# A three-layer max-aggregating graph network: one-hots of layer 1 on VectorE as well, and another price for the lists' picking

## The chip, the cores and the metric

One NeuronCore of a Trainium2 chip runs the kernel. The metric is the device time of one execution in microseconds (us). The time of the kernel before is the median of three runs; the profile is one further execution, taken by the hardware profiler, and times from it are given in us from the start of its span.

## The reference

```
h = max(layernorm(x), 0)                       # 6250 nodes x 128
for Wl, bl, Wr in three layers:                # 128 -> 256 -> 256 -> 128
    agg = segment_max(h[src], dst)             # 200000 edges, sorted by dst; no edge: 0
    h = leaky_relu(agg @ Wl + bl + h @ Wr, 0.01)
out = x + h
```

The destinations are drawn as 6250 u², so low node numbers have many edges and high ones few.

## The kernel before, in words

The 6,250 nodes lie in 50 tiles of 127. An edge's source is a tile and a row in it. The kernel does most of the gathering of source rows as matrix products. For each group of destination nodes (`GROUPS`, five of them, k = 0 to 4) and each pair g of source tiles (25 pairs, from the last to the first), it knows for every destination one source row in that pair, as a byte (`idx_sb`, the same row of bytes on all partitions). A **one-hot** (`hot`) of 128 partitions by up to 1,024 destinations has a 1 where the byte names the partition. TensorE multiplies the tile pair (`pair_sb`) with it and puts the gathered rows into PSUM (`pg`, three buffers); VectorE takes the maximum into the accumulator (`acc`, L956). Edges that don't fit this scheme, a second source in the same pair above all, go to **lists** (k = 0 to 3, of depth 24, 24, 48, 24): GpSimd gathers their rows from DRAM by indirect DMAs (L988, with a pacing memset at L992 behind each), VectorE takes their maxima (L1003, L1008), and the result is fetched when a tile is finished (`agg`, L1033).

**Steps.** The work is one list of steps, 225 of them in layer 1 (called `layer == 0` in the code), 400 in each later layer. A step is one group, one pair, and up to 1,024 destinations. In layer 1 the groups follow each other: steps 0 to 74 are group 0, 75 to 124 group 1 (alternately 1,024 and 384 wide), 125 to 174 group 2, 175 to 199 group 3, all 1,024 wide, and 200 to 224 group 4, 512 wide. A step has two halves, s = 0 and 1, one for each tile of the pair (for groups 1 to 3 each half has its own `pg` and its own maximum). For each half `one_hot` makes, in layer 1, the **distance** `away` = |byte - partition's own number| as bytes (L916), from it the one-hot `relu(1 - away)` (L920), and stores the distance to DRAM in `far` (L922, a DMA on ScalarE's queue), from where the two later layers read it. All three are ScalarE's. There are six `hot` buffers (`HOTS`) and three `away` buffers.

**Order.** The order on each engine is the program's own. The main loop goes over t; it emits the one-hots of step t and the products and maxima of step t - 1. In iteration t there come, in this order: the index words for later gathers (`let`, L977) and the outputs of finished nodes; the first one-hot; the products of half 0 and, for groups 1 to 3, its maximum; the chores and list maxima (`MAXIMA`); the stages of nodes; the gathers and node fetches on GpSimd; the second one-hot; the products and the maximum of half 1. `act(...)` emits what `plan(t, rank, f)` has put down for t.

**Chores.** Layer 1 also prepares what the later groups and lists need, on VectorE, in pieces that `spread` deals over stretches of steps in proportion to a cost given with each piece: `stops` holds the stretches, 0 to 52, 52 to 104, 104 to 140 and 140 to 172. In the second stretch `late_rows(2)` prepares list 2 (16 units, in two parts of 8): masking and flagging each part, **picking** four units at a time (`pick_rows`: MAX8 at L555 and MATCH_REPLACE8 at L557, one round for each 8 of the list's depth), then `rank_rows` (VectorE L569 to L613 with three small products), 16 indirect DMAs on GpSimd that send the picked rows to DRAM (`picks`, L621), and a load of the whole list on SyncE's queue (`ell`, L631). Behind them `late_lookups` makes the bytes of group 2 in fifteen **expansions** (L719 to L726). The list's first gather stands at step 89.

**Nodes.** When group 0 is done, its 24 tiles are finished one a step from step 76 on: `agg` is fetched by GpSimd, `hT_in` by SyncE's queue, three steps later TensorE transposes `agg` (L1049), VectorE merges it (`mz`, L1055), TensorE multiplies by the weights (L1062, L1064), ScalarE copies (L1066, L848, L851), VectorE finishes (L1073, L856). Group 1 follows in the same way from step 126 on, the others after step 200.

Of the kernel before, what the change touches and what calls it, by code (L numbers as in the profile page):

```python
# [38 lines left out]
AF = mybir.ActivationFunctionType  # L39
OP = mybir.AluOpType  # L40
# [20 lines left out]
DEEP = (24, 24, 48, 24)  # L61
# [2 lines left out]
HOT, HOTS = 1024, 6  # L64
AHEAD = 3
EARLY = 44


@with_exitstack
def kernel(ctx: ExitStack, tc: tile.TileContext, x, src, dst,  # L70
                    Wl1, bl1, Wr1, Wl2, bl2, Wr2, Wl3, bl3, Wr3, out):
    nc = tc.nc
# [392 lines left out]
    def rows_of(us):  # L465
        w, i = us[0]
        assert [u for u in us] == [(w, i + j) for j in range(len(us))]
        return {"n": rows_n, "w": rows_w, "x": rows_x}[w][:, i : i + len(us), :]
# [8 lines left out]
    def width_of(us):  # L477
        w, i = us[0]
        ns = {WINDOW[j >= 24] if w == "n" else 2 * CUT if j < NW else CUT for w, j in us}
        return max(ns)  # L480
# [66 lines left out]
    def pick_rows(k, i0, us, S):  # L547

        n, W, m = len(us), width_of(us), DEEP[k]
        whole = S(0, F32, n, W)  # L550
        nc.vector.tensor_copy(whole, rows_of(us)[:, :, :W])
        top = S(2, F32, n, m)
        for i in range(n):
            for o in range(0, m, 8):
                nc.vector.max(out=top[:, i, o : o + 8], in_=whole[:, i, :])  # L555
                if o + 8 < m:
                    nc.vector.match_replace(  # L557
                        out=whole[:, i, :], in_to_replace=top[:, i, o : o + 8], in_values=whole[:, i, :], imm_value=0.0
                    )
        nc.vector.tensor_scalar(picked[k][:, i0 : i0 + n, :], top, -float(LEAF), 0.0, op0=OP.add, op1=OP.max)  # L560
        there = S(0, F32, n, m)
        nc.vector.tensor_scalar(there, top, float(LEAF), None, op0=OP.is_ge)
        nc.vector.reduce_sum(left_n[k][:, i0 : i0 + n], there, axis=AX.X)
# [65 lines left out]
    def load_ell(k):  # L629
        n = len(LISTS[k])  # L630
        nc.sync.dma_start(ell[k], picks[k].rearrange("(p q) m -> p q m", q=n))  # L631
# [141 lines left out]
    wr, wl, bias, bias3 = [], [], [], []  # L773
# [33 lines left out]
    near = keep.tile([P, 2], F32, name="near")  # L807
# [98 lines left out]

    hots, live, done_with = {}, [0], [0, 0]

    def one_hot(layer, k, g, c, w, odd, s):

        t, of = idx_q[layer, k, g]
        put = 2 * c * P + s * w
        if layer == 0:
            at = of + (c + (odd if s else 0) + (NV if PLANES[k][c] in EXTRA else 0)) * P
            away = work.tile([P, HOT], U8, tag="away", name="away", bufs=3)[:, :w]
            nc.scalar.activation(away, t[:, at : at + w], AF.Abs, bias=near[:, s : s + 1], scale=1.0)  # L916
        else:
            away = t[:, of + put : of + put + w]
        hot = work.tile([P, HOT], F32R, tag="hot", name="hot", bufs=HOTS)
        nc.scalar.activation(hot[:, :w], away, AF.Relu, bias=1.0, scale=-1.0)  # L920
        if layer == 0:
            nc.scalar.dma_start(far[k][:, g, put : put + w], away)  # L922
        hots[layer, k, g, c, s] = hot
        live[0] += 1
# [205 lines left out]
    def parts_in(layer, ks):  # L1130

        n = (8 if widths[layer] == P else 4) * P
        parts = []
        for k in ks:
            mine = list(parts_of(k))
            for i, (c0, pw, odd) in enumerate(mine):
                kind = PLANES[k][c0][0]
                cs = []
                for c in range(c0, c0 + pw // P, n // P):
                    w = min(n, (c0 - c) * P + pw)  # L1140
                    cs.append((c - (NV if kind == "x" else 0), w, c, PLANES[k][c][1] if kind == "w" else None))
                parts.append(((i + 0.5) / len(mine), k, (c0, pw, odd), cs))
        return [p[1:] for p in sorted(parts, key=lambda p: p[:2])]

    steps, begins, ends_at, order, blocks, jobs_h = [], [], {}, [], [], []
    for layer in range(3):
        begins.append(len(steps))
        for n, ks in enumerate(PASSES[layer]):
            for g in range(NG - 1, -1, -1):
                order.append((layer, n, g))  # L1150
                of = {}
                for k, (c0, pw, odd), cs in parts_in(layer, ks):
                    if k not in of:
                        if (NG - 1 - g) % GB[k] == 0:
                            blocks.append((layer, k, list(range(g, g - GB[k], -1))))
                        of[k] = max(i for i, b in enumerate(blocks) if b[:2] == (layer, k))
                    jobs_h += [(len(steps), of[k], (layer, k, g, c0, pw, odd, s)) for s in range(2)]
                    for c in cs:
                        steps.append((layer, k, g, c, n))
                        ends_at[layer, k] = len(steps)  # L1160
# [19 lines left out]
    chores = []  # L1180
# [4 lines left out]
    def late_rows(k):  # L1185
        us = LISTS[k]
        i0 = 0
        for part in [[u for u in us if (u in EXTRA_OF) == v] for v in (True, False)]:
            if not part:
                continue  # L1190
            chores.append((2.5, lambda part=part: mask_rows(part, S_acc)))
            chores.append((18 if part[0][0] == "w" else 6, lambda part=part: flag_rows(part, S_acc)))
            for i in range(0, len(part), 4):
                chores.append((7, lambda k=k, i0=i0 + i, p=part[i : i + 4]: pick_rows(k, i0, p, S_acc)))
            i0 += len(part)
        chores.append((7, lambda: rank_rows(k, S_acc, made)))
        for i in range(0, len(us), 4):
            chores.append((0, lambda i=i: [send_row(k, j) for j in range(i, min(i + 4, len(us)))]))

        def load():  # L1200
            load_ell(k)
            listed_at[k] = here_now[0]

        chores.append((0, load))
# [35 lines left out]
    i0 = 0  # L1240
    for i1, t0, t1 in stops:
        spread(chores[i0:i1], t0, t1)
        i0 = i1
# [5 lines left out]
    for layer in range(3):  # L1249
        b0, end = begins[layer], begins[layer + 1]  # L1250
        lists_ = [early_list if (layer, k) == (0, 0) else Listed(layer, k) for k in range(NL)]
        early = 0 if layer else EARLY
        turn = ends_at[layer, 3] - DELAY[layer]
        whens = []
        for part, t0, t1 in ((lists_[:3], max(b0 + 2, rows_at), turn), (lists_[3:], turn, end - 1 - SOON)):
# [5 lines left out]
            early, t = 0, 0  # L1261
# [4 lines left out]
        done_at, i, at = [], 0, 0  # L1266
        for k, li in enumerate(lists_):
            for t in range(len(li.seq)):
                if whens[i] is None:
                    at = 1 + i // 8  # L1270
                else:
                    plan(max(whens[i] - LEAD, 0), LET, lambda li=li, t=t: li.release(t))
                    plan(whens[i], GATHER, lambda li=li, t=t: li.gather(t))
                    at = max(at, whens[i] + (SOON if k == NL - 1 else DELAY[layer]))
# [83 lines left out]
    soon = early_list  # L1358
    for t in range(EARLY):
        soon.release(t)  # L1360
# [16 lines left out]
    for t in range(max(max(agenda)[0] + 1, len(steps) + 1)):  # L1377
# [10 lines left out]
        if t < len(steps):  # L1388
            st = steps[t]
            layer, k, _, _, _ = st  # L1390
            if (layer, k) not in accs:
                i, o = ACC[k]
# [10 lines left out]
        if before_:  # L1403
            p = psum.tile([P, 2, 512], F32, tag="pg", name="pg", bufs=3)
            products(before_[0], 0, p)
            if before_[0][3][3] is not None:
                maxima(before_[0], 0, p, accs[before_[0][:2]])
                p = psum.tile([P, 2, 512], F32, tag="pg", name="pg", bufs=3)
# [8 lines left out]
        if here and (t == 0 or pair_at(t - 1) != pair_at(t)):  # L1417
            i = at_pair[pair_at(t)] + 2
# [288 lines left out]
```

## Time and profile before

| | us |
|---|---|
| median of three runs (lowest, highest) | 3393.74 (3389.39, 3394.82) |
| the profiled execution: time, and its span | 3386.89, 3384.8 |
| busy over the span: PE, DVE, ACT, POOL | 2535.2, 2674.5, 1879.2, 2461.2 |
| layer 1's steps: first distance, last distance | 234.4, 1361.3 |
| ScalarE's distances (x450) and one-hots of layer 1 (x450) | 463.7, 427.7 |

PE is TensorE, PEld its weight loads, DVE VectorE, ACT ScalarE, POOL GpSimd, SP SyncE; a q behind a name is the engine's sequencer, which waits and issues DMAs. A group's row gives the source line, the engine, the operation, output and inputs with their shapes, the count, then the busy time, the mean of one in ns, and how long the engine idled just ahead of them and for whom. A timeline row gives start, duration, engine, line, names, and in brackets the idle time ahead with the releaser. A row of waits gives who waited for whom, the total, the number of times and the longest.

Steps are found in the trace by counting distances, two a step: step 52 begins its distances at about 490 us, step 75 at 610.9, step 125 at 909.5, step 145 at 1013.9, step 200 at 1255.4. VectorE's maximum of a step comes some steps' time behind that where VectorE is late.

### The profile page before, as it was taken

To read this page: it belongs to the slowest core of one execution; us is meant where nothing else is said; L and a number is where in the kernel's file an instruction comes from. 1 tells how busy PE (TensorE), PEld (TensorE's weight loads), DVE (VectorE), ACT (ScalarE), POOL (GpSimd) and SP (SyncE) were. 2 spreads that over 40 slices of the span, in tenths; PEclk is the share of its full clock that TensorE was granted. 3 is DMA by queue.
4 is the path that set the end of the run, shared out by engine and by line. 5 is a ranking of instruction groups with operands and counts; after the bars stand their busy time and mean duration, and the time that the engine had idled before them with its cause. 6 is when DMAs were issued, how large, how long until landed. Compare 5 with 4: busy or idle time off the path is not lost.

```text
span 3384.8 us, 38792 instructions
## 1 busy us (share of the span) xinstructions
PE 2535.2 (75%) x9920; PEld 1833.9 (54%) x9920; DVE 2674.5 (79%) x4157; ACT 1879.2 (56%) x2762; POOL 2461.2 (73%) x3478
## 2 busy tenths in 40 slices
PE   1035664365676667899999989887999999989886
PEld 1023333243454333677777666655777777666654
DVE  6677679777766653699989888884699989999974
ACT  5128897466999996555544434433455545333432
POOL 4788865476867655488888767775388888878782
PEclk9986777587778876899999999998999999999998
DMA  9234554267676677656757767667666756666575
GB/s 303 50 65 135 140 140 134 82 199 195 164 223 172 191 210 206 187 183 199 195 175 187 225 201 226 203 190 241 210 194 194 202 176 179 203 188 206 171 228 166
DMA packets 355527, 620.98 MB, mean 183 GB/s; under 512 B 68694, under 2 KB 216883, under 8 KB 354657
## 3 DMA queue, kind: packets, MB, share of 16 engines
q1 hardware_dynamic: 210561, 367.36, 33.7%
q0 software_dynamic: 79872, 199.22, 24.1%
q10 hardware_dynamic: 64864, 51.83, 4.5%
q8 instruction: 83, 1.36, 0.2%
q14 instruction: 147, 1.20, 0.1%
HBM read 476.03 MB, written 142.13 MB: 183 GB/s over the span
## 4 chain that ended last, share of the span: by engine, by line
PE 28%; DVE 22%; POOL 16%; DMA 12%; issue 11%; ACT 10%; SPq 0%; ACTq 0%; DVEq 0%; POOLq 0%
PE pg L939 21%; DVE acc L956 10%; POOL g L988 9%; ACT away L916 6%; DMA g<-table,let 5%; POOL pace_t L992 3%; ACT hot L920 3%; DVE g L1008 2%; PE z_p L1062 2%; DVE g L1003 2%; PE z_p L1064 2%; POOL picks L621 2%; DMA far<-away 1%; DMA joined<-joined_v 1%; DVE acc L557 1%
## 5 line engine op out<-in xcount | busy, mean ns | idle before, releaser
L939 PE MATMUL pg<-hot,pair_sb 128*128 128x512 f32 x8000 | 2212.9, 426 | 425.3 <-ACT hot L920 191.3
L939 PEld LDWEIGHTS pg<-hot,pair_sb 128*128 128x128 f32 x8000 | 1551.0, 204 | 950.8 <-ACT hot L920 422.2
L988 POOL DMA_INDIRECT g<-table,let x1539 | 1552.1, 1009 | 664.5 <-ACT let L977 291.0
L956 DVE TENSOR_TENSOR acc<-acc,pg 128x1024 f32<-128x1024 f32 (+3 forms) x1439 | 1642.8, 1167 | 415.0 <-PE pg L939 388.7
L920 ACT ACTIVATE hot<-idx_sb 128x1024 fp32r<-128x1024 uint8 (+1 forms) x900 | 817.1, 946 | 552.7 <-PE pg L939 349.2
L992 POOL MEMSET pace_t<- 128x300 bf16 x1539 | 563.0, 366 | 0.8
L916 ACT ACTIVATE away<-idx_sb,near 128x1024 uint8<-128x1024 uint8 (+2 forms) x450 | 463.7, 1030 | 68.4 <-DMA best<-g 17.7
L920 ACT ACTIVATE hot<-away 128x1024 fp32r<-128x1024 uint8 (+2 forms) x450 | 427.7, 950 | 46.0 <-PE pg L939 31.8
L1066 ACT COPY s<-z_p 127x256 f32<-127x256 f32 (+1 forms) x150 | 50.2, 334 | 452.0 <-PE z_p L1064 421.0
L1003 DVE TENSOR_TENSOR g<-g 128x1024 f32<-128x1024 f32 (+5 forms) x218 | 221.4, 1016 | 20.4 <-DMA g<-table,let 20.2
L1033 POOL DMA_INDIRECT agg<-best,end_i x141 | 144.7, 1026 | 106.9 <-PE aT_p L1049 41.2
L1008 DVE TENSOR_TENSOR g<-g 128x512 f32<-128x512 f32 (+3 forms) x351 | 173.1, 493 | 10.5 <-DMA g<-table,let 0.2
L1062 PE MATMUL z_p<-wr,hT_in 128*128 128x256 f32 (+1 forms) x500 | 142.9, 404 | 6.6 <-DMA hT_in<-across 6.6
L1064 PE MATMUL z_p<-wl,mz 128*128 128x256 f32 (+1 forms) x500 | 127.7, 373 | 14.6 <-DVE mz L1055 13.8
L846 PE MATMUL hT_p<-ident,h 128*128 128x128 f32 x200 | 47.9, 326 | 116.2 <-DVE mz L1055 54.1
L977 ACT ACTIVATE let<-ell 128x4 int32<-128x4 int16 (+3 forms) x444 | 81.1, 191 | 79.1 <-DMA ell<-picks 67.7
L848 ACT COPY hT<-hT_p 128x254 f32<-128x254 f32 x100 | 36.7, 367 | 141.5 <-PE hT_p L846 136.6
L1064 PEld LDWEIGHTS z_p<-wl,mz 128*128 128x128 f32 x500 | 91.8, 212 | 32.4 <-DVE mz L1055 22.3
L846 PEld LDWEIGHTS hT_p<-ident,h 128*128 128x128 f32 x200 | 24.6, 158 | 148.2 <-DVE mz L1055 67.1
L1062 PEld LDWEIGHTS z_p<-wr,hT_in 128*128 128x128 f32 x500 | 82.1, 207 | 31.4 <-issue 8.9
L1055 DVE TENSOR_TENSOR mz<-acc,aT_p 128x256 f32<-128x256 f32 (+1 forms) x141 | 52.3, 371 | 58.4 <-PE aT_p L1049 58.3
L621 POOL DMA_INDIRECT picks<-picked,to_i x55 | 57.7, 1050 | 43.0 <-DVE rank_h L597 32.6
(268 smaller groups left out, 1223.2 us busy)
## 6 DMA issues: line engine op xcount, KB each, us to landing
pair_sb<-pair SPq DMA_DIRECT2D x150, 512.0 KB
far<-away ACTq DMA_DIRECT2D x350, 128.0 KB
idx_sb<-far SPq DMA_DIRECT2D x50, 768.0 KB
pair_sb<-pair SPq DMA_DIRECT2D x125, 256.0 KB
pair<-pr SPq DMA_DIRECT2D x100, 256.0 KB
idx_sb<-far SPq DMA_DIRECT2D x50, 512.0 KB
g<-table,let POOLq DMA_INDIRECT x1539
idx_sb<-idx SPq DMA_DIRECT2D x50, 384.0 KB
```

The lines of the kernel that those rows point to most:

```text
L621: s = nc.gpsimd.indirect_dma_start(out=picks[k], out_offset=bass.IndirectOffsetOnAxis(ap=to_i[k][:, i : i + 1], axis=0), in_=picked[k][:, ...
L916: nc.scalar.activation(away, t[:, at : at + w], AF.Abs, bias=near[:, s : s + 1], scale=1.0)
L920: nc.scalar.activation(hot[:, :w], away, AF.Relu, bias=1.0, scale=-1.0)
L939: nc.tensor.matmul(to, pr[:, s, i, kk * P : (kk + 1) * P], hot[:, o : o + bw], start=((alone or s == 0) and i == 0), stop=((alone or s == ...
L956: nc.vector.tensor_max(to, to, of)
L988: nc.gpsimd.indirect_dma_start(out=self.tiles[q, b][:, i, :], out_offset=None, in_=tables[self.layer], in_offset=bass.IndirectOffsetOnAxis ...
L992: nc.gpsimd.memset(pace_t, 0.0)
L1003: nc.vector.tensor_max(base[:, : i + 1, :], base[:, : i + 1, :], g[:, : i + 1, :])
L1008: nc.vector.tensor_max(base[:, :h, :], base[:, :h, :], base[:, w - h : w, :])
L1033: nc.gpsimd.indirect_dma_start(out=self.agg[:, : self.F], out_offset=None, in_=of, in_offset=bass.IndirectOffsetOnAxis(ap=at, axis=0),)
L1062: nc.tensor.matmul(z_p, self.hT[:, i, :], wr[layer][:, i, :], start=False, stop=False)
L1064: nc.tensor.matmul(z_p, self.m[:, i, :], wl[layer][:, i, :], start=False, stop=(i == K - 1))
```

## The change

Two edits. First, in layer 1's steps from `BOTH` = 110 on, in every second step, the one-hot of half 1 is made by VectorE, by comparing the bytes themselves: (byte + near) == 0, where `near` is minus the partition's own number. ScalarE still makes the distance of that half and stores it. Second, a `pick_rows` piece costs 1.2 for each 4 of the list's depth in the dealing, where it cost 7 for all lists: 7.2 for depth 24 and 14.4 for depth 48.

```diff
+BOTH = 110
...
-    def one_hot(layer, k, g, c, w, odd, s):
+    def one_hot(layer, k, g, c, w, odd, s, both):
...
-        nc.scalar.activation(hot[:, :w], away, AF.Relu, bias=1.0, scale=-1.0)
+        if both:
+            nc.vector.tensor_scalar(
+                hot[:, :w], t[:, at : at + w], near[:, s : s + 1], 0.0, op0=OP.add, op1=OP.is_equal
+            )
+        else:
+            nc.scalar.activation(hot[:, :w], away, AF.Relu, bias=1.0, scale=-1.0)
...
-                    jobs_h += [(len(steps), of[k], (layer, k, g, c0, pw, odd, s)) for s in range(2)]
+                    for s in range(2):
+                        both = layer == 0 and s == 1 and len(steps) >= BOTH and len(steps) % 2 == 0
+                        jobs_h.append((len(steps), of[k], (layer, k, g, c0, pw, odd, s, both)))
...
-                chores.append((7, lambda k=k, i0=i0 + i, p=part[i : i + 4]: pick_rows(k, i0, p, S_acc)))
+                chores.append((1.2 * (DEEP[k] // 4), lambda k=k, i0=i0 + i, p=part[i : i + 4]: pick_rows(k, i0, p, S_acc)))
```

58 one-hots move to VectorE: 8 of 384 columns (steps 110 to 124), 37 of 1,024 (126 to 198), 13 of 512 (200 to 224).

On ScalarE, step 180 and the first half of step 181, before:

```order
L916 ACTIVATE away<-idx_sb,near 128x1024
L920 ACTIVATE hot<-away 128x1024
L922 DMA far_159<-away 128x1024
L916 ACTIVATE away<-idx_sb,near 128x1024
L920 ACTIVATE hot<-away 128x1024
L922 DMA far_159<-away 128x1024
L977 ACTIVATE let<-ell_854 128x2
L916 ACTIVATE away<-idx_sb,near 128x1024
```

The same place after (lines below the edit are 6 higher):

```order
L917 ACTIVATE away<-idx_sb,near 128x1024
L926 ACTIVATE hot<-away 128x1024
L928 DMA far_159<-away 128x1024
L917 ACTIVATE away<-idx_sb,near 128x1024
L928 DMA far_159<-away 128x1024
L983 ACTIVATE let<-ell_854 128x2
L917 ACTIVATE away<-idx_sb,near 128x1024
```

One `hot` is gone; the store of the second distance now follows the distance directly.

On VectorE near step 182, before (`g` are a list's gathered rows; ten maxima are five steps):

```order
L1003 TENSOR_TENSOR g<-g 128x512
L1008 TENSOR_TENSOR g<-g 128x512
L1008 TENSOR_TENSOR g<-g 128x256
L1008 TENSOR_TENSOR g<-g 128x128
L956 TENSOR_TENSOR acc_1572<-acc_1572,pg 128x1024 x10
```

After:

```order
L962 TENSOR_TENSOR acc_1572<-acc_1572,pg 128x1024 x4
L1009 TENSOR_TENSOR g<-g 128x512
L1014 TENSOR_TENSOR g<-g 128x512
L1014 TENSOR_TENSOR g<-g 128x256
L1014 TENSOR_TENSOR g<-g 128x128
L922 TENSOR_SCALAR hot<-idx_sb,near 128x1024
L962 TENSOR_TENSOR acc_1572<-acc_1572,pg 128x1024 x4
```

A compare stands behind every fourth maximum, behind the list maxima of its iteration and ahead of the second maximum of the step before.

On GpSimd, at the end of list 2's sends, before (`best` is the list result of group 0, `gap_t` a memset ahead of each send):

```order
L620 MEMSET gap_t 128x1
L621 DMA picks_163<-picked_862,to_i_866 2048x48
L988 DMA g<-table_75,let 128x128
L992 MEMSET pace_t 128x300
L988 DMA g<-table_75,let 128x128
L992 MEMSET pace_t 128x300
L988 DMA g<-table_75,let 128x128
L992 MEMSET pace_t 128x300
L988 DMA g<-table_75,let 128x128
L992 MEMSET pace_t 128x300
L1033 DMA agg<-best_0_140,end_i_856 128x128
```

After, at their beginning:

```order
L1039 DMA agg<-best_0_140,end_i_856 128x128
L994 DMA g<-table_75,let 128x128
L998 MEMSET pace_t 128x300
L994 DMA g<-table_75,let 128x128
L998 MEMSET pace_t 128x300
L1039 DMA agg<-best_0_140,end_i_856 128x128
L621 MEMSET gap_t 128x1
L622 DMA picks_163<-picked_862,to_i_866 2048x48
```

Before, all 16 sends stood ahead of the first of the 24 node fetches; now four fetches (the last of them shown) stand ahead of the sends, and twenty behind. On SyncE's queue the list's load moves in the same way, from ahead of the first `hT_in` to behind the fourth.

The pieces of the second stretch move as follows (step at which each is dealt, worked out from the costs): list 2's first mask and flags stay at 52, its second go from 62 and 63 to 65 both; its four picks from 58, 60, 69, 71 to 57, 61, 70, 74; its rank from 73 to 78; its sends and load from 75 to 80; the fifteen expansions from 75 ... 101 to 80 ... 101. In the other stretches only the sends, the load and the first expansion of list 1 move, from step 18 to 19.

## Prediction

> **What bounds the kernel now.** The change touches layer 1 alone, which ends near 1,376 us of the span. I first cut the span into stretches (busy time by stretch; the columns are PE, PEld, DVE, ACT, POOL in us, the granted clock, the DMA share and GB/s).
>
> ```profile
> core 0: us, PE busy (x) PEld busy (x) DVE busy (x) ACT busy (x) POOL busy (x), PEclk, DMA share, GB/s
> 515.00:648.00 133.00, 62.42 (x187) 45.34 (x188) 120.81 (x373) 92.48 (x106) 62.03 (x95) 0.68 0.35 104
> 648.00:676.00 28.00, 12.68 (x36) 8.60 (x36) 15.19 (x33) 5.64 (x11) 24.01 (x35) 0.54 0.45 126
> 676.00:833.00 157.00, 96.62 (x350) 64.67 (x348) 120.59 (x261) 102.39 (x184) 106.76 (x149) 0.81 0.72 198
> 910.00:1014.00 104.00, 80.86 (x259) 52.07 (x258) 76.43 (x131) 95.53 (x127) 73.82 (x104) 0.77 0.69 210
> 1014.00:1255.00 241.00, 163.85 (x450) 95.03 (x450) 154.56 (x230) 234.05 (x255) 161.40 (x243) 0.83 0.67 191
> 1255.00:1376.00 121.00, 80.83 (x210) 44.28 (x210) 44.32 (x91) 78.24 (x151) 61.29 (x81) 0.63 0.69 191
> 1376.00:3385.00 2009.00, 1791.03 (x7701) 1364.76 (x7699) 1719.98 (x1879) 899.32 (x1424) 1529.53 (x2168) 0.97 0.66 198
> ```
>
> Two stretches have a bound that the change moves. From 1,014 to 1,255 ScalarE is busy 234 of 241 us. From 515 to 648 VectorE is busy 121 of 133. The last row, 59% of the span, is untouched. Next come the instructions of 1,014 to 1,255 (ScalarE's byte distances by source line; VectorE's maxima by group) and who waited there.
>
> ```profile
> L916 ACT ACTIVATE away<-idx_sb,near x110: 1131/1133/1147, 1013.9 to 1253.2; 128x1024 uint8<-128x1024 uint8 x110
> L956 DVE TENSOR_TENSOR acc<-acc,pg 128x1024 f32<-128x1024 f32 x93 | 113.5, 1220 | 80.0 <-PE pg L939 78.4
> PEld pg L939 <- ACT hot L920: 124.8, 102, 3.3
> PE pg L939 <- ACT hot L920: 71.0, 80, 2.9
> POOL g L988 <- ACT let L977: 58.4, 23, 6.7
> ```
>
> A step makes two distances, so 110 of them are 55 steps, 145 to 199, at 241 / 55 = 4.38 us each. TensorE waits 71 us for one-hots, VectorE 78 for TensorE, GpSimd 58 for ScalarE's index lists: all three wait for ScalarE in the end.
>
> **What ScalarE gets back.** A job, half a step, is a distance, its store to `far`, and a one-hot (timeline of ScalarE; ACTq is its sequencer issuing a DMA):
>
> ```profile
> 1122.12 1.13 ACT L916 ACTIVATE away<-idx_sb,near 128x1024 uint8<-128x1024 uint8 x1
> 1123.29 1.06 ACT L920 ACTIVATE hot<-away 128x1024 fp32r<-128x1024 uint8 x1
> 1123.30 0.33 ACTq L922 DMA_DIRECT2D far<-away  x1
> 1124.25 1.13 ACT L916 ACTIVATE away<-idx_sb,near 128x1024 uint8<-128x1024 uint8 x1
> 661.87 0.35 ACTq L922 DMA_DIRECT2D far<-away  x1
> 662.26 0.61 ACT L916 ACTIVATE away<-idx_sb,near 128x384 uint8<-128x384 uint8 x1 [12.83 <-DMA pair_sb<-pair]
> ```
>
> The job takes 1124.25 - 1122.12 = 2.13 us, of which the one-hot adds 1124.25 - 1123.29 = 0.96. That is not all won. The store's issue (0.33 us) now runs beneath the one-hot. Without it the store waits for the distance, and the next distance waits for the store's issue: the last two rows show an activation that starts 0.39 us after such an issue began. So a job without its one-hot takes 1.17 + 0.39 = 1.56 us and wins 0.57, not 0.96. If the sequencer could pass the store, it would be 0.96; I take 0.57, since the row shows the order.
>
> A one-hot moves in every even step from 110. Steps 126 to 198 hold 37 of full width: 27 in 1,014 to 1,255 and 10 in 910 to 1,014. The first stretch wins 27 x 0.57 = 15.4 us; I keep 13.5, as some of it will meet a full buffer or a late maximum. In 910 to 1,014 the node steps make VectorE and ScalarE both links of one chain, so 10 x 0.57 = 5.7 is mostly eaten by the compares (below): I take 1. The 8 narrow moves before 126 (384 columns) and the 13 after 199 (512) have one-hots about as short as the store's issue, and after 1,255 no engine is full: nothing. Sum: 14.5 us won, with ends 0 and 37 x 0.96 = 35.5.
>
> **What VectorE takes on.** No instruction of before compares bytes. The nearest rows are a compare of as many f32 elements with a scalar per partition (L665) and the maximum above, 1.22 us at one element per cycle. A third row shows what GpSimd does to such a single-source instruction (all three columns are min/median/max ns).
>
> ```profile
> L665 DVE TENSOR_SCALAR under<-iota_r,ve x3: 747/803/817, 165.5 to 169.8; 128x1024 f32<-128x1024 f32 x3
> L719 DVE TENSOR_SCALAR acc<-rows_w x40: 273/286/851, 675.9 to 826.4; 128x512 int16<-128x512 int16 x40
> ```
>
> I take 0.80 us plus 0.1 for meetings with GpSimd, 0.9, with ends 0.75 and 1.3. In 1,014 to 1,255 that adds 27 x 0.9 = 24 us to 154.6, 179 of the 227 us that are left: cover enough, unless the order bites. It can: a compare stands on VectorE's queue behind the step's chores and list maxima and ahead of the second maximum of the step before, and TensorE's second half of the step waits for it. Buffers for three steps of one-hots lie between. In 910 to 1,014 it adds 9 to 76, there on the node chain; hence the 1 us above.
> The Trainium skill, "SBUF — State Buffer", section "Who interferes with whom", says that a VectorE instruction using both port pairs and a GpSimd instruction exclude each other, the later one blocking fully. L719's spread, 273 to 851 ns, agrees; by the rule a compare could start up to a GpSimd instruction late, or hold up a gather's issue. GpSimd is busy 161 of 241 us, so the second costs nothing here.
>
> **What the dealing moves.** List 2 is the one of depth 48; its picking is now counted twice as long. Its rank and the first expansion of its rows leave the stretch that VectorE fills (VectorE timeline: rank's first and last instruction; one expansion, and the maximum behind it):
>
> ```profile
> 625.94 0.97 DVE L569 TENSOR_TENSOR acc<-down,left_n 128x784 f32<-128x784 f32 x1
> 636.05 0.20 DVE L613 TENSOR_REDUCE over<-sums 128x1 f32<-128x48 f32 x1
> 647.87 1.14 DVE L719 TENSOR_SCALAR acc<-rows_w 128x512 int16<-128x512 int16 x5
> 651.19 3.46 DVE L956 TENSOR_TENSOR acc<-acc,pg 128x384 f32<-128x384 f32 x4
> PE pg L939 <- DVE acc L956: 37.9, 5, 13.6
> ACT hot L920 <- PE pg L939: 31.8, 5, 18.4
> ```
>
> Rank goes from step 73 to 78 (10.3 us), the expansion (3.3) from 75 to 80: 13.6 us less. The four picks, 13 to 14 us each, stand four steps apart where two pairs stood two apart, and four steps are 17 us of ScalarE's work, so a pick fits between. The stretch falls from 133 towards 120, not under the 24 x 4.26 = 102 that ScalarE needs. The last two rows (waits, 515 to 676) are the stalls that shrink. I take 10 of the 13.6.
>
> Given back later: rank now lies in 648 to 676, where VectorE idles half the time because of this (GpSimd, SyncE, TensorE timelines):
>
> ```profile
> 635.28 1.01 POOL L621 DMA_INDIRECT picks<-picked,to_i  x1 [32.55 <-DVE rank_h L597]
> 656.20 1.18 POOL L988 DMA_INDIRECT g<-table,let  x1 [0.30 <-issue]
> 657.10 0.32 SPq L631 DMA_DIRECT2D ell<-picks  x1
> 667.64 0.48 PE L1049 MATMUL aT_p<-ident,agg 128*128 128x128 f32 x1 [14.79 <-DMA agg<-best,end_i]
> ```
>
> GpSimd waits for rank, sends 16 rows in 21 us, and only then fetches the first node; SyncE's queue stands behind the list's load; TensorE loses 14.8 us and ScalarE 12.8 (row above, its `pair_sb` load behind the same queue). Afterwards four fetches stand ahead of the sends. The fifth lands about 21 + 3 + 6 = 30 us behind rank, and its merge comes five steps behind rank, some 25 us at this pace: a stall of about 5 in place of 14.8. That pays for rank, 10.3, so this stretch comes out even. But I count 3 us for what queues behind the sends. From step 80 on all fifteen expansions remain where twelve did: 3 x 3.3 = 10 us more VectorE work in 676 to 833, where it idles 36 of 157; I take 4. Dealing: -10 + 3 + 4 = -3 us, with ends -14 and +12.
>
> **Sum.** -14.5 - 3 = -17.5 us. The profiled execution took 3386.9 us (span 3384.8), 6.9 less than the median of three, 3393.7; the difference carries over, so 3393.7 - 17.5 = 3376 us.
>
> **Rivals.**
> - *The store's issue costs nothing* (0.12). ScalarE wins 0.96 a job and the dealing its 14: 0.9 x 35.5 + 10 = 42 us, 3352. Against it: the row at 661.87.
> - *VectorE cannot take the compares* (0.20). At 1.3 us, 27 x 1.3 = 35 us make VectorE 190 of 227, and with the chores in bursts TensorE waits for the compare as long as it waited for ScalarE; 14.5 goes to 0 and the dealing leaves -3: 3391, no change. For it: VectorE's order. Against: in 1,014 to 1,255 VectorE never waits for a gather, only for TensorE.
> The Trainium skill, "VectorE: DVE Perf Modes", section "Mode 2×_2P — use both read ports for one tensor", lets one source in SBUF run at two elements a cycle and names no element size. By its 0.96 GHz that is 0.53 us plus a fixed part, an estimate; L665 agrees for f32, no row shows bytes.
> - *The sends land among the node fetches* (0.14; the slower side). Before, they delay one node; now twenty node fetches follow them on GpSimd, at 106.8 of 157 us already, and 21 us come in: 128. If the fifth fetch comes later than some 20 us behind its merge, the delay runs through all of them: +21 for the sends and +10 for the expansions against -13.6, and with 5 us of the compares' gain left, 3394 + 17 - 5 = 3406. Against it: GpSimd no longer sits 32 us waiting for rank with fetches behind it.
>
> **Chances.** My forecast has 0.52; 0.02 is left for none of these. A measurement can tell about 0.2%, 7 us, from no change. Faster: nearly all of the forecast (0.50), the first rival (0.12), a little of the second (0.03) make 0.65. Same: most of the second and the edges, 0.19. Slower: the third rival and the tail of the second, 0.16. The range runs from the first rival's end, 3351, to 3400, which takes in the second and leaves most of the third out.
>
> **What would show it.** After: distances followed at once by a store start the next activation about 1.56 us later (0.57 right) or 1.17 (first rival); compares at L922 take 0.8 to 0.9 us; steps 145 to 199 take about 227 us; TensorE's wait for VectorE's `hot` stays under 10 us in all (else the second rival); the first agg wait of 14.8 us is gone and none over 10 follows (else the third); VectorE's full stretch ends near step 75 some 10 us earlier. I am wrong if ScalarE drops well under 97% in steps 145 to 199 and the steps are no shorter.

## The result, and the profile after

| | before | after |
|---|---|---|
| median of the runs (lowest, highest), us | 3392.65 (3388.34, 3403.67), 6 runs | 3375.83 (3363.98, 3382.62), 6 runs |
| ratio after / before, 95% interval | | 0.995 (0.9933, 0.9968) |
| the profiled execution: time, and its span, us | 3386.89, 3384.8 | 3363.98, 3362.2 |

The change makes the kernel 16.8 us faster by the medians, and 11 to 23 us by the interval of the ratio; the forecast was 17.5. The profiled execution of after is the shortest of its six runs, so its span shows somewhat more.

Busy time by stretch, after; the columns are those of the prediction's first view, the stretches are cut at the same steps.

```profile
core 0: us, PE busy (x) PEld busy (x) DVE busy (x) ACT busy (x) POOL busy (x), PEclk, DMA share, GB/s
515.00:635.00 120.00, 59.86 (x181) 42.08 (x182) 109.51 (x346) 89.10 (x102) 68.65 (x101) 0.70 0.45 128
635.00:665.00 30.00, 18.09 (x51) 11.85 (x52) 25.22 (x56) 14.15 (x23) 15.28 (x27) 0.61 0.26 76
665.00:826.00 161.00, 98.85 (x340) 65.85 (x339) 121.89 (x265) 97.15 (x176) 108.04 (x150) 0.73 0.69 193
903.00:1005.00 102.00, 72.86 (x260) 48.74 (x259) 81.46 (x141) 86.28 (x116) 74.78 (x103) 0.84 0.70 215
1005.00:1237.00 232.00, 155.17 (x453) 97.44 (x451) 176.44 (x259) 209.64 (x228) 168.22 (x245) 0.82 0.70 200
1237.00:1355.00 118.00, 76.19 (x209) 44.11 (x210) 49.20 (x104) 70.41 (x137) 61.00 (x80) 0.66 0.68 193
1355.00:3362.00 2007.00, 1787.54 (x7700) 1360.71 (x7698) 1719.76 (x1879) 899.60 (x1424) 1526.16 (x2168) 0.97 0.65 198
```

Steps 145 to 199 take 232 us instead of 241. ScalarE is busy 210 of them, 90% where it was 97%, VectorE 176 where it was 155. The stretch that VectorE fills is 120 us long instead of 133, and VectorE has 110 of work in it. The last row, the two later layers, is within 2 us of before.

Who waited in steps 145 to 199, after (total us, times, longest):

```profile
PEld pg L945 <- ACT hot L926: 106.4, 74, 2.8
PE pg L945 <- ACT hot L926: 67.9, 67, 2.4
DVE acc L962 <- PE pg L945: 49.5, 49, 2.7
POOL g L994 <- ACT let L983: 43.9, 22, 7.3
PEld pg L945 <- DVE hot L922: 5.4, 4, 4.3
PE pg L945 <- DVE hot L922: 3.6, 1, 3.6
```

ScalarE is still waited for by TensorE and GpSimd. VectorE's wait for TensorE falls from 78 to 50 us, while the compares bring it 22 us of work (27 of 0.82 us); TensorE waits for a compare in five places, 9 us in all.

Two moved jobs on ScalarE, after (timeline; ACTq is its sequencer): one with a distance behind it, one with an index list (`let`).

```profile
1129.75 1.13 ACT L917 ACTIVATE away<-idx_sb,near 128x1024 uint8<-128x1024 uint8 x1
1130.91 0.33 ACTq L928 DMA_DIRECT2D far<-away  x1
1131.28 1.15 ACT L917 ACTIVATE away<-idx_sb,near 128x1024 uint8<-128x1024 uint8 x1 [0.40 <-ACT away L917]
...
1145.89 1.13 ACT L917 ACTIVATE away<-idx_sb,near 128x1024 uint8<-128x1024 uint8 x1
1147.05 0.35 ACTq L928 DMA_DIRECT2D far<-away  x1
1147.59 0.21 ACT L983 ACTIVATE let<-ell 128x4 int32<-128x4 int16 x1 [0.56 <-DMA g<-table,let]
1147.70 1.13 ACT L917 ACTIVATE away<-idx_sb,near 128x1024 uint8<-128x1024 uint8 x1
```

The store waits for the distance, and ScalarE stands still while it is issued: 0.40 us idle in the first job, 0.56 in the second (the releaser named there, a gather, is the last semaphore seen; the issue just before is what ScalarE itself was doing). The first job takes 1.53 us from distance to distance, the second 1.81.

The dealing, after: GpSimd's timeline at the first send,

```profile
647.29 1.00 POOL L622 DMA_INDIRECT picks<-picked,to_i  x1 [22.41 <-DVE rank_h L598]
```

and rows of the waits from 640 to 830 us:

```profile
DVE mz L1061 <- PE aT_p L1055: 12.4, 9, 4.2
ACT s L1072 <- DMA ell<-picks: 7.2, 1, 7.2
PE aT_p L1055 <- DMA agg<-best,end_i: 3.4, 1, 3.4
```

GpSimd waits 22 us for the rank where it waited 33, and TensorE's wait of 14.8 us for a node's `agg` is down to 3.4. VectorE's waits for the nodes' transposes come to 12.4 us, where the stretch from 640 to 835 us of before has 19.3, and ScalarE has one of 7.2 for list 2's load.

**By steps.** Since the steps are the same in all kernels here, the end of VectorE's last maximum of a step, found by counting maxima in each trace, tells where time goes. (Of group 2's steps, 125 to 174, only every second one has a maximum for each half, as the kernel's description says of all of them; in the even ones both halves share one. That makes 325 maxima in layer 1.) The first row is before, in us; the others are differences from it. Group 0 ends with step 74, layer 1 with step 224; compares stand from step 110 on, in the last two rows from 145, and in "dealing only" nowhere. Kernels that are alike up to a step differ there by up to 5 us, but the way from one step to another repeats better: the nine kernels that are alike from 75 to 105 give back 6.5 to 8.7 us there.

| step | 60 | 75 | 85 | 100 | 105 | 144 | 199 | 224 | median, us from before |
|---|---|---|---|---|---|---|---|---|---|
| before | 556.4 | 647.5 | 719.1 | 811.8 | 839.3 | 1017.1 | 1258.8 | 1375.3 | |
| after | +1.4 | -12.8 | -18.5 | -6.1 | -6.1 | -7.3 | -18.5 | -21.2 | -16.8 |
| compares only | -0.9 | -1.3 | -1.0 | -1.0 | -1.0 | +1.0 | -9.9 | -12.4 | -9.0 |
| dealing only | +0.1 | -13.9 | -19.6 | -7.2 | -7.1 | -8.3 | -10.5 | -10.4 | -8.4 |
| store behind | +1.6 | -12.2 | -18.0 | -4.6 | -4.5 | -7.4 | -33.9 | -36.4 | -36.9 |
| fourth buffer | +1.9 | -12.7 | -18.5 | -5.4 | -5.3 | -6.7 | -20.7 | -26.0 | -22.3 |
| every step | +2.2 | -11.5 | -17.3 | -4.5 | -4.4 | -0.6 | -20.8 | -19.6 | -19.2 |
| compares twice | +1.5 | -11.7 | -17.5 | -4.6 | -5.2 | +5.9 | -3.3 | -3.2 | -1.1 |
| three expansions less | +3.9 | -10.3 | -15.9 | -14.7 | -10.2 | -7.5 | -18.6 | -20.0 | -19.6 |
| every step, behind | +1.5 | -13.0 | -18.8 | -5.2 | -5.8 | -4.3 | -37.9 | -43.3 | -37.9 |
| from 145, every second | +0.1 | -13.6 | -19.4 | -7.1 | -7.0 | -8.0 | -19.1 | -20.4 | -16.7 |
| from 145, every step, behind | +1.4 | -11.6 | -16.7 | -2.9 | -2.9 | -6.6 | -41.7 | -44.5 | -46.9 |

Each median is set against runs of the kernel before on the same chip. Behind step 224 the instructions are those of before, and one profiled execution differs there from another by up to 18.6 us; so layer 1 is read from the steps and the whole from the medians.

### The profile page after: what moved, and what is told of

The parts are those of the page before. It is cut to its first block, busy times and chain, and to the rows that moved or that the text cites. A ratio compares the mean times of both kernels' runs of the same rounds, so it can differ in the third digit from the quotient of the medians.

```text
span 3362.2 us, 38834 instructions
## 1 busy us (share of the span) xinstructions
PE 2513.2 (75%) x9919; PEld 1828.9 (54%) x9920; DVE 2709.0 (81%) x4215; ACT 1834.2 (55%) x2704; POOL 2466.1 (73%) x3478
## 3 DMA queue, kind: packets, MB, share of 16 engines
q1 hardware_dynamic: 210561, 367.36, 33.9%
## 4 chain that ended last, share of the span: by engine, by line
PE 27%; DVE 23%; POOL 16%; DMA 14%; issue 10%; ACT 9%; SPq 0%; ACTq 0%; DVEq 0%; POOLq 0%
PE pg L945 21%; DVE acc L962 11%; POOL g L994 9%; DMA g<-table,let 6%; ACT away L917 5%; POOL pace_t L998 3%; DVE g L1014 2%; ACT hot L926 2%; DVE g L1009 2%; PE z_p L1068 2%; PE z_p L1070 2%; DMA far<-away 2%; POOL picks L622 2%; DMA agg_v<-best,end_i 1%; DMA joined<-joined_v 1%
## 5 line engine op out<-in xcount | busy, mean ns | idle before, releaser
L917 ACT ACTIVATE away<-idx_sb,near 128x1024 uint8<-128x1024 uint8 (+2 forms) x450 | 464.1, 1031 | 79.9 <-DMA best<-g 31.1
L926 ACT ACTIVATE hot<-away 128x1024 fp32r<-128x1024 uint8 (+2 forms) x392 | 376.1, 960 | 12.5
L1009 DVE TENSOR_TENSOR g<-g 128x1024 f32<-128x1024 f32 (+5 forms) x218 | 221.5, 1016 | 22.8 <-DMA g<-table,let 22.5
L1039 POOL DMA_INDIRECT agg<-best,end_i x141 | 143.7, 1019 | 107.3 <-PE aT_p L1055 44.5
L1014 DVE TENSOR_TENSOR g<-g 128x512 f32<-128x512 f32 (+3 forms) x351 | 173.1, 493 | 10.5 <-issue 0.2
L1070 PE MATMUL z_p<-wl,mz 128*128 128x256 f32 (+1 forms) x500 | 126.2, 370 | 14.1 <-DVE mz L1061 13.5
L1070 PEld LDWEIGHTS z_p<-wl,mz 128*128 128x128 f32 x500 | 90.5, 208 | 31.1 <-DVE mz L1061 21.2
L1068 PEld LDWEIGHTS z_p<-wr,hT_in 128*128 128x128 f32 x500 | 82.0, 207 | 36.2 <-issue 12.5
L352 POOL DMA_INDIRECT win_d<-in_dst_dram,win_i x50 | 54.0, 1081 | 44.3 <-ACT junk_w L357 13.9
```

The lines of the kernel that those rows point to most:

```text
L1009: nc.vector.tensor_max(base[:, : i + 1, :], base[:, : i + 1, :], g[:, : i + 1, :])
L1014: nc.vector.tensor_max(base[:, :h, :], base[:, :h, :], base[:, w - h : w, :])
L1039: nc.gpsimd.indirect_dma_start(out=self.agg[:, : self.F], out_offset=None, in_=of, in_offset=bass.IndirectOffsetOnAxis(ap=at, axis=0),)
L1068: nc.tensor.matmul(z_p, self.hT[:, i, :], wr[layer][:, i, :], start=False, stop=False)
L1070: nc.tensor.matmul(z_p, self.m[:, i, :], wl[layer][:, i, :], start=False, stop=(i == K - 1))
```

## The experiments

**The two edits apart.** Compares only: the old price of 7 for the picking. Dealing only: no step is late enough for a compare.

```diff
-                chores.append((1.2 * (DEEP[k] // 4), lambda k=k, i0=i0 + i, p=part[i : i + 4]: pick_rows(k, i0, p, S_acc)))
+                chores.append((7, lambda k=k, i0=i0 + i, p=part[i : i + 4]: pick_rows(k, i0, p, S_acc)))
```

> The compares alone, with the old dealing (7 for every pick). If a moved one-hot shortens ScalarE's queue by about 0.5 us, steps up to 110 run as before, steps 126 to 144 win some 2 us, steps 145 to 199 some 10 us, and the time falls by 12 to 15 us (0.4%) against before. If VectorE cannot take the compares, or the gain of the changed kernel came from the dealing, the time is that of before within 4 us.

```diff
-BOTH = 110
+BOTH = 1000
```

> The new dealing alone, no compares. If the expansions that were pushed into the node stretch give the gain back, step 75 ends 13 us earlier than before, step 80 about 18, step 110 only 6, and that is what stays: 6 us or 0.2% faster. If it was the compares from step 110 on that lost what the dealing had won, 18 us stay. If the sends among the node fetches delay the rest, it is slower than before.

Compares only: 3382.63 us against 3391.63, ratio 0.9967 (0.9957, 0.9977). Dealing only: 3383.27, ratio 0.9983 (0.9972, 0.9995). The savings of the medians, 9.0 and 8.4 us, add up to 17.4, the change's own 16.8; at the end of layer 1 it is 12.4 + 10.4 = 22.8 against 21.2. The edits show no sign of helping or hurting each other. The forecast had them at 14.5 and 3. The ratios, which are not those of the medians, put the compares at 11.2 us (7.8 to 14.6) and the dealing at 5.8 (1.7 to 9.5). So the compares come out below the 12 to 15 us that were expected, though steps 144 to 199 win 10.9 us where some 10 were expected; of the dealing, about the 6 us that were expected stay.

**The store behind the next one-hot.** The store of a job without a one-hot is kept until ScalarE has made the next one-hot, and issued beneath it; a fourth distance buffer holds the waiting one.

```diff
-            away = work.tile([P, HOT], U8, tag="away", name="away", bufs=3)[:, :w]
+            away = work.tile([P, HOT], U8, tag="away", name="away", bufs=4)[:, :w]
...
-            nc.scalar.dma_start(far[k][:, g, put : put + w], away)
+            held.append((far[k][:, g, put : put + w], away))
+        if not both:
+            for to, what in held:
+                nc.scalar.dma_start(to, what)
+            held.clear()
```

> The changed kernel, but the store of a distance whose one-hot VectorE makes is issued behind the next one-hot on ScalarE, and there is a fourth buffer for distances. If the exposed issue of the store costs 0.5 us each time, the next distance starts 1.17 us behind the last instead of 1.62 to 1.69, 37 x 0.47 = 17 us are in play and 8 to 14 of them come out against the changed kernel (3362 to 3368 us at its median of 3376). If ScalarE is no longer the bound there, or VectorE sets the pace, the time stays at that of the changed kernel.

Measured: 3354.75 us, ratio 0.9884 (0.9865, 0.9902), 20 us below the changed kernel as measured from before (36.9 against 16.8), more than the 8 to 14 expected. ScalarE's timeline in this kernel, a moved job with an index list behind it:

```profile
1143.83 1.14 ACT L918 ACTIVATE away<-idx_sb,near 128x1024 uint8<-128x1024 uint8 x1
1144.87 0.19 ACT L988 ACTIVATE let<-ell 128x2 int32<-128x2 int16 x1
1144.97 1.13 ACT L918 ACTIVATE away<-idx_sb,near 128x1024 uint8<-128x1024 uint8 x1
1146.13 1.06 ACT L927 ACTIVATE hot<-away 128x1024 fp32r<-128x1024 uint8 x1
1146.14 0.85 ACTq L932 DMA_DIRECT2D far<-away  x2
```

Both stores, 0.85 us, run beneath one one-hot, and the idle time is gone: the job takes 1.14 us instead of 1.81. From 1,005 to 1,237 us ScalarE is back at 94% (busy time by stretch; its own steps 145 to 199 end at 1,221 us, and up to there it is 207 of 217, 95%):

```profile
1005.00:1237.00 232.00, 157.03 (x477) 99.94 (x476) 183.81 (x271) 218.75 (x249) 177.42 (x257) 0.85 0.76 212
```

Counted over steps 145 to 199 of the three traces, from a distance to the next, medians:

| job | before | after | store behind |
|---|---|---|---|
| with one-hot; then a distance | 2.13 | 2.13 | 2.13 |
| with one-hot; then `let` | 2.22 | 2.22 | 2.22 |
| without; then a distance (8 times) | | 1.62 | 1.04 |
| without; then `let` (19 times) | | 1.80 | 1.14 |

So the 27 moved one-hots win 8 x 0.51 + 19 x 0.42 = 12.1 us in after, and with the store behind 8 x 1.09 + 19 x 1.08 = 29.2. The table by steps, from 144 to 199, has 11.2 and 26.5. That the exposed issue is what the change fails to win is shown, if the buffer is not the cause:

> The changed kernel with a fourth buffer for the distances, and nothing else; the stores stay where the change put them. It parts the two edits of the kernel that stores behind the next one-hot. Theory (the exposed issue of the store is what a moved one-hot fails to win, and the fourth buffer only makes room for a store that comes later): within 4 us of the changed kernel, and a distance that follows a distance still starts 1.62 to 1.69 us behind it. Rival (the distances wait for a buffer): 10 to 20 us below the changed kernel, as the kernel that stores behind.

Measured, with the first of the two edits above alone: 3366.22 us against 3388.55, ratio 0.9947 (0.9927, 0.9966), which is no different from the change's 0.995 within the intervals. Steps 144 to 199 win 14.0 us, 2.8 more than the change, and the steps after them 2.6 more. Together that is above the 4 us of the expectation, but far from 15. It is the rival's part: ScalarE's distances wait 4.0 us for the buffers that stores still read in steps 145 to 199 of after, and 0.7 here. A distance behind a distance without a one-hot still starts 1.59 us later (median of 8; 1.62 in after). The other 12.5 us of steps 144 to 199 are the store's place.

**The compare in every step.**

```diff
-                        both = layer == 0 and s == 1 and len(steps) >= BOTH and len(steps) % 2 == 0
+                        both = layer == 0 and s == 1 and len(steps) >= BOTH
```

> The changed kernel with a compare in every step from 110 on instead of every second. If VectorE has room, ScalarE's steps 145 to 199 lose another 28 x 0.47 = 13 us, VectorE's busy time there rises by 28 x 0.82 = 23 to 199 of some 220 us, and 4 to 10 us of it come out against the changed kernel. If VectorE's order is what limits, as the second rival had it, TensorE's waits for VectorE's one-hots rise from 4 us to tens and the time is that of the changed kernel or worse.

Measured: 3372.39 us, ratio 0.9935 (0.992, 0.995), against the change's 0.995: no clear gain, and layer 1 ends 1.6 us later. The rival holds: TensorE's matmuls wait 15.5 us for compares from 1,010 to 1,235 us and 31.1 from 850 to 1,010. But the steps show two halves. From 144 to 199 twice as many moves win 20.2 us instead of 11.2; from 105 to 144, 3.8 us are lost where the change won 1.2, and the rest goes in the tail.

**Each compare made twice.**

```diff
+            for _ in range(2):
+                nc.vector.tensor_scalar(
+                    hot[:, :w], t[:, at : at + w], near[:, s : s + 1], 0.0, op0=OP.add, op1=OP.is_equal
+                )
```

> The changed kernel with each of the 58 compares made twice into the same buffer: it doubles what VectorE takes on and leaves ScalarE's gain alone. 58 compares are some 37 x 0.82 + 21 x 0.48 = 40 us more of VectorE. Theory (in steps 145 to 199 VectorE has the cover, 176 of 232 us busy; in 110 to 144 the nodes make it a link of the chain): steps 145 to 199 within 4 us of the changed kernel's, 3 to 6 us lost before step 145, the whole 3 to 10 us above the changed kernel. Rival (VectorE's order bites, TensorE's second half waits for the compare): steps 145 to 199 lose 10 us or more, and the whole is back at the kernel before or above it.

Measured: 3387.44 us, ratio 1.0 (0.9984, 1.0016); 15.7 us of the change's 16.8 are gone. The busy time of this kernel from 860 to 1,010 and from 1,005 to 1,237 us:

```profile
860.00:1010.00 150.00, 96.84 (x318) 63.94 (x318) 123.77 (x212) 116.07 (x158) 106.13 (x147) 0.77 0.63 186
1005.00:1237.00 232.00, 154.87 (x445) 96.88 (x444) 201.21 (x294) 205.39 (x224) 175.57 (x241) 0.81 0.67 194
```

TensorE's wait for the compare from 860 to 1,010 us, here,

```profile
PE pg L946 <- DVE hot L923: 23.1, 7, 8.0
```

and in after:

```profile
PE pg L945 <- DVE hot L922: 17.5, 6, 6.1
```

By the whole time the rival is right, by the place it is not. From step 144 to 199, where the doubling adds 25 us to VectorE (201 of 232 busy, 176 in after), the kernel wins 9.2 us where the change wins 11.2: the cover is there. From 105 to 144 it loses 11.1 us where the change wins 1.2, though the doubling adds only 12.4 us to VectorE's busy time there (154.8 us between the ends of these two steps, 142.4 in after): the full price. VectorE is not full there, 82% of 189 us. So in the stretch of the nodes a compare lies on the path; behind it, it does not.

**Compares only from step 145 on.** Both kernels set `BOTH = 145`; the second also has the store behind, the fourth buffer and the compare in every step. That combination from step 110 on was run first.

> The kernel that stores behind the next one-hot, and the compare in every step from 110 instead of every second: both edits that by themselves beat or equalled the changed kernel. Theory (a moved one-hot wins about 0.75 us where the store is covered, until another engine becomes the bound; with 75 wide compares VectorE comes to some 205 to 215 of what would be 205 us in steps 145 to 199): VectorE and the node chain take over, so it is within 8 us of the kernel that stores behind, either side, and VectorE is over 90% busy in steps 145 to 199. Rival (ScalarE stays the bound): 15 to 25 us below that kernel, about 3335.

> The changed kernel with the compares of every second step only from step 145 on, where it had them from 110; the stores and the buffers as the change has them. I had counted 1 us for the ten full-width compares of steps 126 to 144 and nothing for the eight narrow ones before. Theory (there they pay on VectorE what they win on ScalarE): within 3 us of the changed kernel at the end of layer 1, and within 4 in the whole. Rival (they win 0.47 us each, as from step 145 on): 5 to 8 us above the changed kernel.

> Stores behind the next one-hot, the fourth buffer, and the compare in every step, but only from step 145 on (from 110 in the kernel that stores behind in every step). Between 110 and 144 that kernel lost some 3 us against the changed kernel, and doubled compares lost 10 there. Theory (before step 145 a compare stands on the chain of the nodes and wins nothing; behind it each wins): steps 110 to 144 come back by 2 to 4 us and the rest stays, so layer 1 ends 45 to 48 us before that of the kernel before, the whole 2 to 5 us below the kernel with every step from 110, about 3346. Rival (the compares before 145 do win, and their time is only seen later): 5 us or more above that kernel.

Every step, behind, from 110: 3350.7 us against 3388.55, ratio 0.9894 (0.9873, 0.9915). Every second from 145: 3374.96 against 3391.66, ratio 0.9948 (0.9934, 0.9962). Every step, behind, from 145: **3344.81**, ratio 0.9859 (0.9844, 0.9875), the fastest here, 46.9 us below the kernel before. In that last kernel, steps 145 to 199 (up to the last maximum, at 1,217 us) by busy time,

```profile
1005.00:1218.00 213.00, 146.03 (x461) 94.16 (x461) 200.01 (x291) 184.03 (x208) 183.60 (x247) 0.86 0.78 221
```

the group of its compares (count, busy us, mean ns, idle before),

```profile
L923 DVE TENSOR_SCALAR hot<-idx_sb,near 128x1024 fp32r<-128x1024 uint8 x55 | 49.6, 902 | 0.0
```

and two of TensorE's waits:

```profile
PE pg L950 <- DVE hot L923: 39.7, 29, 5.1
PEld pg L950 <- ACT hot L927: 37.9, 35, 2.3
```

The compares of steps 110 to 144 win nothing when they are every second (105 to 144: -1.0 us without, -1.2 with them) and cost 5 us when they are all (-3.7 without, +1.5 with). Behind step 145 the bound has moved: VectorE is 94% busy, ScalarE 86%, and TensorE's matmuls wait 40 us for VectorE's compare, where they waited 3.6 in after. The theory of the first expectation holds: with every step from 110 the kernel is 37.9 us below before, where every second, behind, has 36.9, and VectorE is busy 197 of the 210 us of its steps 145 to 199; from 144 to 199 it wins 33.6 us instead of 26.5, and has lost 4.4 us of these 7.1 between 105 and 144. So does that of the second (-20.4 at the end of layer 1 against -21.2, 16.7 us in the whole against 16.8). That of the third holds in part: from 105 to 144 it is 5.2 us better than its first form, but layer 1 ends 44.5 us before that of the kernel before, only 1.2 us better. By the medians the whole is 9 us better and not 2 to 5; the steps do not show where the rest comes from, and no run here tells.

**Three expansions less.**

```diff
             def part(g0=g0):
                 if g0 == 0:
                     got[0] = made.tile([P, len(us), NG], I16, tag="least", name="least", bufs=2)
+                if us[0][0] == "x" and g0 >= 2 * BATCH:
+                    if g0 == 2 * BATCH:
+                        nc.vector.memset(got[0][:, :, g0:], PAST)
+                    return
```

> The changed kernel without three of group 2's fifteen expansions: the last three of its extra part, dealt to about steps 95 to 101, are replaced by one memset, so that some edges of group 2 are left out. It measures what an expansion costs in the stretch of the nodes, where I had put 4 us for three and the trace of after gave back some 12. Theory (there an expansion is about 4.2 us of VectorE and lies on the path with nearly all of it): step 110 ends 9 to 13 us earlier than in the changed kernel, and the whole time is 6 to 13 us lower. Rival (they fit into VectorE's idle time, as I had mostly counted): step 110 at most 4 us earlier.

Measured: 3368.97 us against 3388.55, ratio 0.9947 (0.9928, 0.9966): the whole is not measurably lower than the change's. The busy time from 782 to 808 us, in this kernel and, below it, in after:

```profile
782.00:808.00 26.00, 19.94 (x77) 13.25 (x78) 15.12 (x30) 20.58 (x38) 19.76 (x29) 0.83 0.88 222
```

```profile
782.00:808.00 26.00, 16.19 (x51) 10.26 (x50) 20.57 (x44) 16.13 (x29) 17.20 (x25) 0.70 0.73 181
```

Without them TensorE gets through 77 products instead of 51, and step 100 ends 8.6 us earlier than in after: there VectorE's expansions are the pace, at nearly their full price. Counting that this kernel came 2.5 us later to step 75, it is 11. By step 110 the lead is 2.4 us (-9.4 against -7.0), and by 144 it is gone. What eats it between 100 and 125 these runs do not settle. Neither expectation holds whole: the price is the theory's, the effect on the end is the rival's.

## Why the prediction was right, by its own steps

- **A moved one-hot wins less than it takes, by its store.** Right, and mis-sized: 0.57 us predicted, 12.1 / 27 = 0.45 measured. Where a distance follows, the 1.56 us forecast stand against a median of 1.62 (the shortest is 1.53). But behind 19 of the 27 moved jobs stands a `let`, and that costs more behind an issue (0.56 us idle) than behind a one-hot; the prediction had not looked at what follows the store. From step 145's first distance to step 200's it is 231.7 us instead of 241.4, not 227: -9.8, or -11.2 by VectorE's maxima, where the term was -13.5.
- **The first rival** (the store's issue costs nothing) is refuted by the 0.40 and 0.56 us of idle time. Its price was good: with the store covered, 26.5 us come in where it said 27 x 0.96 = 25.9, though some 2.8 of them are the fourth buffer's.
- **The compare at 0.9 us.** Measured 0.82 (22.1 us of 27 in steps 145 to 199), between the ends 0.75 and 1.3:

```profile
L922 DVE TENSOR_SCALAR hot<-idx_sb,near x27: 744/780/1306, 1011.1 to 1228.1; 128x1024 fp32r<-128x1024 uint8 x27
L922 DVE TENSOR_SCALAR hot<-idx_sb,near x18: 410/746/1091, 851.4 to 1003.9; 128x1024 fp32r<-128x1024 uint8 x10, 128x384 fp32r<-128x384 uint8 x8
L922 DVE TENSOR_SCALAR hot<-idx_sb,near x13: 477/481/916, 1237.2 to 1340.8; 128x512 fp32r<-128x512 uint8 x13
```

The fastest of 384, 512 and 1,024 columns take 410, 477 and 744 ns, 0.52 ns an element beside a fixed 0.21 us. The Trainium skill, "VectorE: DVE Perf Modes", section "Mode 2×_2P — use both read ports for one tensor", promises two elements a cycle; by the page's 0.96 GHz that is 0.521 ns an element, an estimate, and these rows agree with it for bytes compared into fp32r.

- **VectorE's cover.** Right from step 145 on: 176 us busy where 179 were forecast, and doubling the compares costs 2 us. Before 145 the 1 us of gain was in truth none. The runs show the price there, not what sets it: VectorE is busy only 142 of 177 us from step 105 to 144 in after, and TensorE's matmuls, which wait 26 us for ScalarE's one-hots there without compares (every second from 145), wait 18 for them and 20 for VectorE's compares with them. So the order on VectorE is at least part of it; the node chain that the prediction named is not shown apart from it. The sign I had named for the second rival, more than 10 us of TensorE's waits for the compare in all, did come: 17.5 us of it from 860 to 1,010 alone. That rival's mechanism exists in 110 to 144, and the kernel with doubled compares shows its price; in 145 to 199, where it was placed, it does not decide.
- **The dealing, -10 + 0 + 3 + 4 = -3.** The direction of the -10 and of the +4 was right, the sizes not. With the start of the stretch as zero (step 60), after is 14.2 us ahead at step 75, 19.9 at 85, and 7.5 at 100. The first number is about the 13.6 us of moved work, where I took 10. Much of the next is only put off: when step 85 ends, before has done seven of the fifteen expansions and after five, and an expansion takes some 4 us here, not 3.3. From 85 to 100 it is given back, 12.4 us where I had 4 + 3. That leaves 7.5, and 8.4 in the whole for the dealing alone (5.8 by the ratio). What pays, by the traces, is the `agg` stall that is gone and makes room for the rank, and the picks that no longer come in pairs; no run tried these apart. Of the two stalls that the prediction named, TensorE's for VectorE's maxima only falls from 37.9 to 34.6 us (515 to 665 in after); ScalarE's 31.8 us for TensorE is gone, but ScalarE now stands still twice, for 10.0 and 11.2 us, which the profile puts down to stores of list results. The 3 us for queues behind the sends do not show, apart from the one wait of 7.2 us for the list's load.
- **The third rival** (sends among node fetches) is absent: no `agg` wait over 10 us follows; the one that TensorE has is 3.4.
- **The tail, counted at nothing**, brings 2.7 us from step 199 to 224, 2.5 with the compares alone and nothing with the dealing alone (+0.1). The kernels with the same 13 compares there win 1.3 to 5.3. That is at the edge of what the steps can tell; if it is real, the 512-wide one-hots shorten something there.
- **The sum.** The compares were put at 14.5 and measure 9.0 in the whole (11.2 by the ratio, 12.4 at the end of layer 1); the dealing was put at 3 and measures 8.4 (5.8 by the ratio, 10.4 at the end of layer 1). That the total is right to a microsecond is luck: these two errors cancel, and the interval of the result alone is 12 us wide.

## What to carry to other kernels

When an instruction leaves the engine that sets the pace, look at what had been running beneath it: here a DMA's issue of 0.33 us came into the open and took 17 of the 29 us that the move could win by the jobs' medians, and putting it beneath the next instruction, with a buffer more, brought 20 us, in a kernel where the move itself had brought 9. Ask for each stretch apart whether the engine that takes the work has cover: a second run of the same compare was nearly free behind step 145 and cost its full time in the stretch before. A lead in the middle of a stretch may be work put off: count what each kernel has done by then before calling it a gain.

## What the runs showed of the hardware that was not expected

- ScalarE's own DMA issue blocks it. Each takes 0.33 to 0.36 us and in the rows above the next activation starts 0.04 us (a distance) or 0.19 us (a `let`) behind it. The Trainium skill, "DMA: Bandwidth & Descriptors", section "Issuing engines are not separate DMA queues", says that the time to initiate a DMA "is usually small relative to the DMA itself". Here what counts is not the DMA but the engine: 27 such issues on the engine that sets the pace cost 12.5 us by the steps and 17 by the jobs, so the rule is no ground to leave them uncounted.
- Two distances that do not depend on each other start 1.04 us apart, though the profile shows each as 1.13 long; a one-hot that reads the distance starts 1.17 us behind it. So a job without its one-hot wins up to 1.09 us, more than the 0.96 by which the one-hot lengthened it.
- The mean of a full-width compare is larger where GpSimd is busier: 819 ns where GpSimd is busy 168 of 232 us, 902 where it is 184 of 213. Two means are not a proof that the one causes the other.
